# A selective-scan layer in front of an attention layer: softplus as ln(1 + exp), a new order of the steps' parts, and the second layer's weights loaded earlier

## The chip, the cores and the metric

The kernel runs on one core of a Trainium2 chip. The metric is the device time of one execution in microseconds; for the kernel before it is the median of three runs. A profile is one further execution, recorded instruction by instruction. Engines are named as in the profile: PE is the matrix engine, PEld its weight load, DVE the vector engine, ACT the scalar engine with its function tables, POOL the general engine, SP the engine that issues the DMAs. [...]

## The reference, cut to what matters

All arrays are float32. `x` has 4 images of 384 channels and 64 x 64 pixels.

```python
# layer 0: group norm, layer norm, a Mamba block, residual
xz = xn @ in_proj_w.T;  xb, z = split(xz)             # 384 -> 2 * 768
xc = silu(causal_conv4(xb) + conv_b)                  # per channel, 4 taps
x_dbl = xc @ x_proj_w.T                               # 24 (dt), 16 (B), 16 (C)
dt = softplus(x_dbl_dt @ dt_w.T + dt_b)
h = exp(dt * A) * h + (dt * xc) * B                   # 768 channels x 16 states, over 4096 pixels
y = (sum_n(h * C) + xc * D) * silu(z)
x = x + y @ out_proj_w.T
# layer 1: group norm, outlook attention, residual
a = softmax((avgpool2(xg) @ attn_w.T + attn_b) * scale)   # 12 heads, 9 x 9
v = conv_w[k] @ patches                                # 9 taps, stride 2
x = x + fold(a @ v) @ proj_w.T + proj_b
```

Since softplus(v) is ln(1 + e^v), the third line from `xc` can be had from either.

## The kernel before

The first layer cuts each image's 4096 pixels into 17 chunks of 241 (the last has 240), 68 chunks in all. A chunk has 12 units (`NU`), a unit being two groups of 32 channels with their 16 states each, laid out over 128 partitions. The main loop of `mamba_layer` goes over steps `s`; in step `s` unit `s` is scanned, and every unit's work is spread over the steps around it:

- `s_fetch(s + 4)`, in even steps: SP fetches dt and dt * xc, replicated over partitions, for two units, out of DRAM (`dtd`, `dxd`).
- `s_inputs2(s + 1)`: DVE multiplies half of the inputs by B (`bp`, in PSUM). `s_inputs(s + 2)`: POOL does the other half.
- `s_gate(s - 3)`, in even steps: DVE multiplies the finished output `y` into `zs`. `y` has one PSUM buffer, so the next pair of units may only write it after this.
- `s_scan(s, 0)` and `s_scan(s, 1)`: DVE's two scans. `s_decay(s + 1, 0)` and `(s + 1, 1)`: ACT's four exps each, into the PSUM tile that the scan of that number has just read. `s_carry(s + 1)`: ACT copies the carried state into `h`. `s_save(s)`: DVE saves the state.
- `s_outputs(s - 1)`: POOL multiplies `h` by C. `s_sum(s - 2)`: PE adds over the states, and in the first of two units also xc * D.

Around this the dense parts of other chunks are issued. Those ahead of the scan are named `f_...` (load, layer norm, projections `f_x` and `f_z`, `f_conv`, the silus in `f_gates`, `f_bc` and `f_xd` for x_dbl, `f_dt`, the softplus, `f_dtx`), those after it `e_...` (load of the residual, three output projections, store). Where each stands is written out by hand in two tables, `plan` (line 440) and `ends` (line 465): the key is a step relative to the chunk and one of six places in the step, EARLY, READY, SCAN, POOL, MID, LATE. A chunk's own units are scanned in relative steps 24 to 35, so relative step 13 falls into step 1 of the chunk before, -11 into step 1 as well, and so on; in what follows, steps are numbered 0 to 11 in this sense. A part's instructions go to the end of each engine's queue at its place. In `f_x`, `f_z`, `f_conv`, `f_dt` and `e_project` the matmuls and the ACT instruction that empties the PSUM tile are issued together, so ACT waits for PE if PE isn't done. All these matmuls share one PSUM tag of two buffers (`mm`).

ACT needs a table of functions for each of silu, softplus and exp; where the next function isn't in the loaded table, an ACT_TABLE_LOAD is put ahead of it.

The second layer, `outlook_layer`, runs when the first is done. It loads its own weights at its start (lines 726 to 731) into a pool that it opens there, then goes over 32 tiles of 8 rows.

Of the kernel before, what the change touches and what calls it, by code (L numbers as in the profile page):

```python
# [10 lines left out]
P = 128  # L11
C = 384
# [12 lines left out]
KK = 9  # L25
GW = 11


# [55 lines left out]
@with_exitstack  # L84
def mamba_layer(ctx, tc, x, w, x1, sc1, bi1, consts):

# [17 lines left out]
    small = ctx.enter_context(tc.tile_pool(name="small", bufs=2))  # L104
    io = ctx.enter_context(tc.tile_pool(name="io", bufs=3))
    front = ctx.enter_context(tc.tile_pool(name="front", bufs=1))
    cross = ctx.enter_context(tc.tile_pool(name="cross", bufs=2))
# [7 lines left out]

    def load(name, shape):
        t = wp.tile(shape, F32, tag=name, name=name)
        sp.dma_start(t, w[name])
        return t
# [10 lines left out]
    def x_load(b, i):  # L130
        if i == 0:
            xstats[b] = small.tile([P, NCB, NX, 6], F32, tag="xst", name="xst", bufs=1)
        xs = io.tile([P, NCB, XT], F32, tag="xt", name="xs")
        sp.dma_start(xs, x[b, :, i * XT : (i + 1) * XT].rearrange("(p cb) l -> p cb l", cb=NCB))
        return xs
# [35 lines left out]

    avg = load("avg", [P, P])
    for i in range(NX):
# [5 lines left out]

    onesc = load("onesc", [P, 1])  # L180
    lnw = load("lnw", [P, NCB])
    lnb = load("lnb", [P, NCB])
    win = load("win", [P, NCB, 2 * DI])
    cw = load("cw", [P, NJ, KC])
    cbias = load("cbias", [P, NJ])
    wx = load("wx", [P, NJ, 2 * NS + RK])

    KX = 2 * NS + RK + 1
    xd = wp.tile([2 * CG, TM], F32, tag="xd", name="xd")
    gp.memset(xd, 1.0)  # L190
    wdt = wp.tile([KX, DI], F32, tag="wdt", name="wdt")
    sp.dma_start(wdt[2 * NS :, :], w["wdt"])
# [4 lines left out]

    cdiag = wp.tile([P, NJ, KC, P], F32, tag="cdiag", name="cdiag")
    ddiag = wp.tile([P, NJ, P], F32, tag="ddiag", name="ddiag")
# [5 lines left out]

    sel = wp.tile([2 * NS, NG // 2, P], F32, tag="sel", name="sel")
    sp.dma_start(sel, w["sel"])
    pw = pmm.tile([P, 2, TM], F32, tag="mm", name="pw")
    for j in range(2 * NJ):
        for cb in range(NCB):  # L210
# [6 lines left out]
            )  # L217
    bxz = wp.tile([P, 2 * NJ], F32, tag="bxz", name="bxz")
# [3 lines left out]
    cws = wp.tile([P, NJ], F32, tag="cws", name="cws")  # L222
    ve.reduce_sum(cws, cw, AX.X)
    ve.tensor_mul(cws, cws, bxz[:, :NJ])
    ve.tensor_add(cbias, cbias, cws)
    pad = wp.tile([P, NJ], F32, tag="pad", name="pad")
# [17 lines left out]
    def f_load(c):  # L244
        c.xt = io.tile([P, NCB, XT], F32, tag="xt", name="xt")
# [125 lines left out]
    def f_gates(c):  # L371
        t = c.t
        ae.activation(c.xc[:, :, :t], c.xc[:, :, :t], AF.Silu)
        ae.activation(c.zs[:, :, :t], c.zs[:, :, :t], AF.Silu)

    def f_bc(c):
# [29 lines left out]
    def f_softplus(c):  # L406
        t = c.t
        ae.activation(c.dt[:, :, :t], c.dt[:, :, :t], AF.Softplus)
        c.bc = []
        for k in range(2):  # L410
            m = cross.tile([P, NG, TM], F32, tag=f"bc{k}", name=f"bc{k}")
            for r in range(4):
                sp.dma_start(
                    m[CG * r : CG * (r + 1), :, :t], c.bcd[k, :, r, :t].unsqueeze(0).to_broadcast([CG, NG, t])
                )
            c.bc.append(m)
        c.dtd = dram.tile([NJ, P, TM], F32, tag="dtd", name="dtd")
        sp.dma_start(c.dtd[:, :, :t].rearrange("j p t -> p j t"), c.dt[:, :, :t])

# [44 lines left out]

    ends = {
        (-3, MID): [lambda c: e_load(c)],
        (2, LATE): [lambda c: e_project(c, 0)],
        (4, LATE): [lambda c: e_project(c, 1)],
        (5, LATE): [lambda c: e_project(c, 2)],
        (8, READY): [lambda c: e_store(c)],  # L470
    }

    def parts(s, when):

        for k in range(s // NU + 3, s // NU - 2, -1):
# [133 lines left out]
    def e_load(c):  # L609
        c.xr = io.tile([P, NCB, XT], F32, tag="xr", name="xr", bufs=2)  # L610
        sp.dma_start(
            c.xr[:, :, : c.t], x[c.b, :, c.t0 : c.t0 + c.t].rearrange("(p cb) l -> p cb l", cb=NCB)
        )

    def e_project(c, cb):
# [5 lines left out]
        ae.copy(c.xr[:, cb, :t], po[:, 0, :t])  # L621

    def e_store(c):
# [5 lines left out]
        sp.dma_start(x1[c.b, :, c.t0 : c.t0 + t].rearrange("(p cb) l -> p cb l", cb=NCB), c.xr[:, :, :t])  # L629
        if c.t0 + t == L:  # L630
# [7 lines left out]

    pending = {}
    for s in range(-3 * NU, NU * (len(chunks) + 2)):  # L640
        k, m = divmod(s, NU)
# [20 lines left out]
        for i in range(2):  # L662
            if (u := unit(s)) is not None:
                s_scan(u, i)
            if i == 1:
                parts(s, SCAN)
                if u is not None:
                    s_save(u)
            if (u := unit(s + 1)) is not None:
                s_decay(u, i)  # L670
                if i == 0:
                    s_carry(u)
        if (u := unit(s - 1)) is not None:
            s_outputs(u)
# [8 lines left out]
        if u is not None and u.first:  # L683
            s_sum(u)
        parts(s, LATE)


@with_exitstack
def outlook_layer(ctx, tc, x1, w, out, sc1, bi1, consts):

# [21 lines left out]

    wp = ctx.enter_context(tc.tile_pool(name="wp1", bufs=1))
    io = ctx.enter_context(tc.tile_pool(name="io1", bufs=3))
# [4 lines left out]
    pt = ctx.enter_context(tc.tile_pool(name="pt", bufs=1, space=bass.MemoryType.PSUM))  # L719

    def load(name, shape):
        t = wp.tile(shape, F32, tag=name, name=name)
        sp.dma_start(t, w[name])
        return t
# [8 lines left out]
    ve.tensor_scalar_mul(wa, wa, 0.25)  # L733

# [239 lines left out]


@with_exitstack
def layers(ctx, tc, w, out):
# [16 lines left out]
    consts = (blk12, ident, eps, one)  # L994
    mamba_layer(tc, x.rearrange("b c h w -> b c (h w)"), w, x1, sc1, bi1, consts)
    outlook_layer(tc, x1, w, out, sc1, bi1, consts)

# [65 lines left out]
```

## Time and profile before

| | |
|---|---|
| time, median of 3 runs | 7237.03 us (7232.6 to 7237.15) |
| the profiled execution's own time | 7234.33 us |
| its span, from first to last instruction | 7232.5 us |
| busy: PE, DVE, ACT, POOL | 6332.4, 5651.4, 4972.4, 5426.5 us |
| mean granted PE clock | 0.912 |
| first scan, last scan pair | 139.1 us, 5925.9 us |
| table loads | 272, 1283 ns in the mean |

In the profile's lines of groups and waits, an output stands before `<-` and its inputs behind it, with buffer numbers left out; `h<-da,h` is the scan, `h<-st` the carry, `st` the saved state, `dt<-dt` the softplus. Lines of the program are of no use for telling instructions apart here, since all are recorded in one helper (L40). In a line of waits the numbers are the total in us, how often, and the longest. In a line of the timeline they are the start and the length in us, and a bracket at the end says how long the engine had been idle and what released it. A line of windows gives the stretch, its length, then busy us of PE, PEld, DVE, ACT and POOL with the number of instructions in parentheses, the granted PE clock, the DMA engines' busy share and GB/s.

### The profile page before, as it was taken

The numbers are of one execution on the slowest core, as the hardware profiler recorded it, in microseconds if no ns is written. First come the engines' busy times: TensorE is split into PE (matmuls) and PEld (weight loads), VectorE is DVE, ScalarE is ACT, GpSimd is POOL, SyncE is SP. The second block draws the span as 40 slices with busy tenths as digits, with TensorE's granted clock in tenths as the row PEclk, the third lists the DMA queues.
The fourth block names the chain that finished last, engine by engine and source line by source line (L and its number), as shares of the span: only waits on it lengthen the run. The fifth ranks groups of instructions, "written<-read, shape, count | busy, mean of one in ns | idle before, by whom it ended". The sixth has DMA issues, their size and how long they took to land.

```text
span 7232.5 us, 112296 instructions
## 1 busy us (share of the span) xinstructions
PE 6332.4 (88%) x40440; PEld 4261.8 (59%) x40440; DVE 5651.4 (78%) x5688; ACT 4972.4 (69%) x10729; POOL 5426.5 (75%) x2102
## 2 busy tenths in 40 slices
PE   6888888888888888888888888888888858999999
PEld 5566666566566666566566665566566634555555
DVE  4888888889888888888888888888888874444544
ACT  3777777777777777777777777777777754554454
POOL 3888888888888888888888888888888872433343
PEclk9889899898898999889889999889889979999999
DMA  4555444444554444444554444444554434445444
GB/s 115 127 125 125 114 113 106 116 110 121 126 128 112 117 109 106 117 117 120 126 123 112 114 109 106 111 113 110 117 119 111 110 104 150 164 167 173 163 162 151
DMA packets 899555, 893.17 MB, mean 123 GB/s; under 512 B 121706, under 2 KB 858780, under 8 KB 898485
## 3 DMA queue, kind: packets, MB, share of 16 engines
q1 hardware_dynamic: 898996, 886.00, 47.5%
q8 instruction: 318, 5.21, 0.3%
q14 instruction: 241, 1.97, 0.1%
HBM read 659.99 MB, written 225.68 MB: 122 GB/s over the span
## 4 chain that ended last, share of the span: by engine, by line
PE 54%; DVE 24%; ACT 13%; issue 4%; DMA 2%; POOL 2%; SPq 0%; DVEq 0%; ACTq 0%; POOLq 0%
DVE h L40 19%; PE y L40 14%; PE ps_in L40 11%; PE ps_cv L40 8%; ACT da L40 6%; PE psv L40 5%; PE ps_out L40 4%; PE pso L40 4%; PE ps L40 3%; PE psa L40 2%; POOL h L40 2%; ACT L40 2%; ACT xc L40 2%; ACT zs L40 1%; PE ps_dt L40 1%
## 5 line engine op out<-in xcount | busy, mean ns | idle before, releaser
L40 POOL TENSOR_TENSOR h<-h,bc 128x1928 f32<-128x1928 f32 (+1 forms) x816 | 3229.7, 3958 | 828.1 <-DVE st L40 661.0
L40 DVE TENSOR_TENSOR_SCAN h<-da,h 128x968 f32<-128x968 f32 (+1 forms) x1632 | 3451.8, 2156 | 505.4 <-ACT h L40 480.5
L40 ACT ACTIVATE da<-dtr,aneg 128x241 f32<-128x241 f32 (+1 forms) x6528 | 3038.2, 465 | 658.1 <-DVE h L40 362.1
L40 POOL TENSOR_TENSOR h<-dxr,bc 128x964 f32<-128x964 f32 (+1 forms) x816 | 1685.0, 2065 | 12.6 <-DMA dxr<-dxd 11.2
L40 PE MATMUL y<-h,ssum 128*32 128x241 f32 (+1 forms) x13056 | 1638.2, 410 | 0.6 <-POOL h L40 0.6
L40 PEld LDWEIGHTS y<-h,ssum 128*32 128x32 f32 x13056 | 736.5, 120 | 796.7 <-issue 438.4
L40 PE MATMUL ps_in<-u,win 128*128 128x241 f32 (+1 forms) x4896 | 1073.4, 373 | 5.5 <-DVE u L40 4.8
L40 POOL TENSOR_TENSOR bd<-ain,own 99x1188 f32<-99x1188 f32 x192 | 412.8, 2178 | 791.7 <-DMA ain<-ad 618.9
L40 PEld LDWEIGHTS ps_in<-u,win 128*128 128x128 f32 x4896 | 923.8, 192 | 140.1 <-issue 60.3
L40 DVE TENSOR_TENSOR h<-dxr,bp 128x964 f32<-128x964 f32 (+1 forms) x816 | 940.3, 1152 | 51.9 <-PE bp L40 31.8
L40 PE MATMUL y<-xc,ddiag 128*128 128x241 f32 (+1 forms) x816 | 327.8, 490 | 557.7 <-DVE zs L40 557.7
L40 PE MATMUL ps_cv<-xb,cdiag 128*128 128x241 f32 (+1 forms) x3264 | 718.1, 373 | 1.2 <-ACT xc L40 1.2
L40 PEld LDWEIGHTS ps_cv<-xb,cdiag 128*128 128x128 f32 x3264 | 601.7, 189 | 120.2 <-ACT da L40 51.4
L40 PE MATMUL psv<-wv,xp 128*128 128x384 f32 x1728 | 587.9, 492 | 0.9 <-ACT vst L40 0.8
L40 PE MATMUL ps_out<-zs,wout 128*128 128x241 f32 (+1 forms) x2448 | 585.7, 392 | 0.0
L40 PEld LDWEIGHTS y<-xc,ddiag 128*128 128x128 f32 x816 | 159.5, 229 | 665.2 <-issue 466.9
L40 PEld LDWEIGHTS ps_out<-zs,wout 128*128 128x128 f32 x2448 | 508.9, 208 | 51.7
L40 ACT ACTIVATE bd<-ain,own 99x324 f32<-99x324 f32 x704 | 334.6, 555 | 294.3 <-PE ps L40 282.6
L40 DVE TENSOR_TENSOR fold<-fold,ps 128x192 f32<-128x192 f32 (+1 forms) x768 | 211.2, 303 | 336.2 <-PE ps L40 323.0
L40 PEld LDWEIGHTS psv<-wv,xp 128*128 128x128 f32 x1728 | 320.5, 190 | 224.4 <-issue 7.8
L40 PE MATMUL ps_dt<-xd,wdt 25*128 25x241 f32 (+1 forms) x816 | 270.8, 478 | 166.8 <-ACT xd L40 166.8
L40 ACT ACTIVATE zs<-ps_in,bxz 128x241 f32<-128x241 f32 (+1 forms) x408 | 166.0, 459 | 329.5 <-PE ps_in L40 329.5
(98 smaller groups left out, 5385.3 us busy)
## 6 DMA issues: line engine op xcount, KB each, us to landing
dxr<-dxd SPq DMA_DIRECT2D x1536, 120.5 KB
dtr<-dtd SPq DMA_DIRECT2D x1536, 120.5 KB
bc<-bcd SPq DMA_DIRECT2D x512, 120.5 KB
vin<-vd SPq DMA_DIRECT2D x384, 148.5 KB
vd<-vst SPq DMA_DIRECT2D x96, 576.0 KB
dtd<-dt SPq DMA_DIRECT2D x64, 723.0 KB
dxd<-dtx SPq DMA_DIRECT2D x64, 723.0 KB
xs<-in_x SPq DMA_DIRECT2D x64, 384.0 KB
```

What stands on the lines that cost most here:

```text
L40: return self.tc.keep_in_program_order(issue(*args, **kwargs))
```

## The change

Four things change.

1. `f_dt` evacuates its PSUM tiles with Exp in place of a copy, and `f_log`, in place of the softplus, takes ln(dt + 1). A table set that has both exp and ln (`EXP_LN`) is loaded behind the silus and stays until the next ones.
2. `plan` and `ends` have other places. The loads of B and C for a chunk (`bc0`, `bc1`) stand in a part of their own, `f_spread`; the store of dt goes with the log. `e_load` comes 7 steps earlier.
3. In each step the carry is issued ahead of the first decay.
4. The pools that only the fronts use (`wf`, `iof`, `front`) stand on the right side of the memory and are closed in step `front_end`, the last before the last chunk's scan. From that step on each step issues one DMA of the second layer's weights, ten in all (`behind`), into the room that came free. `outlook_layer` gets them ready.

```diff
@@ f_gates
         ae.activation(c.xc[:, :, :t], c.xc[:, :, :t], AF.Silu)
         ae.activation(c.zs[:, :, :t], c.zs[:, :, :t], AF.Silu)
+        ae.preload_act_table_set(EXP_LN)
@@ f_dt
-        ae.copy(c.dt[:, 2 * jj : 2 * jj + 2, :t], pp[:, :, :t])
-
-    def f_softplus(c):
-        t = c.t
-        ae.activation(c.dt[:, :, :t], c.dt[:, :, :t], AF.Softplus)
+        ae.activation(c.dt[:, 2 * jj : 2 * jj + 2, :t], pp[:, :, :t], AF.Exp)
+
+    def f_log(c):
+
+        t = c.t
+        ae.activation(c.dt[:, :, :t], c.dt[:, :, :t], AF.Ln, bias=one)
+        c.dtd = dram.tile([NJ, P, TM], F32, tag="dtd", name="dtd")
+        sp.dma_start(c.dtd[:, :, :t].rearrange("j p t -> p j t"), c.dt[:, :, :t])
+
+    def f_spread(c):
+
+        t = c.t
         c.bc = []
...
-        c.dtd = dram.tile([NJ, P, TM], F32, tag="dtd", name="dtd")
-        sp.dma_start(c.dtd[:, :, :t].rearrange("j p t -> p j t"), c.dt[:, :, :t])
@@ plan
-        (-12, MID): [f_load],
-        (-11, MID): [f_mean],
-        (-10, READY): [f_center],
-        (-10, LATE): [f_square],
-        (-7, LATE): [f_var],
-        (-6, EARLY): [f_root],
-        (-6, POOL): [f_pow],
-        (-5, MID): [f_rs],
-        (-5, LATE): [f_scale],
-        (7, MID): [at(f_x, 0)],
-        (8, LATE): [at(f_x, 1), at(f_z, 0)],
-        (9, LATE): [at(f_x, 2), at(f_z, 1)],
-        (10, LATE): [at(f_conv, 0)],
-        (11, LATE): [at(f_conv, 1), at(f_z, 2)],
-        (12, LATE): [at(f_conv, 2), f_gates],
-        (14, MID): [f_bc],
-        (14, LATE): [f_xd],
-        (15, LATE): [at(f_dt, 0), at(f_dt, 1)],
+        (-12, READY): [f_load],
+        (-11, SCAN): [f_mean],
+        (-11, POOL): [f_center],
+        (-8, EARLY): [f_square],
+        (-8, LATE): [f_var],
+        (-7, MID): [f_root],
+        (-5, EARLY): [f_pow],
+        (-5, READY): [f_rs],
+        (-5, POOL): [f_scale],
+        (6, POOL): [at(f_x, 0)],
+        (7, POOL): [at(f_conv, 0)],
+        (7, MID): [at(f_z, 0)],
+        (8, SCAN): [at(f_x, 1)],
+        (9, LATE): [at(f_z, 1)],
+        (10, SCAN): [at(f_x, 2)],
+        (10, LATE): [at(f_z, 2)],
+        (12, READY): [at(f_conv, 1)],
+        (12, MID): [at(f_conv, 2)],
+        (13, POOL): [f_gates],
+        (14, LATE): [f_bc],
+        (15, EARLY): [f_xd],
+        (16, EARLY): [at(f_dt, 0)],
+        (16, READY): [at(f_dt, 1)],
         (16, LATE): [at(f_dt, 2)],
-        (17, LATE): [f_softplus],
-        (18, SCAN): [f_dtx],
-        (22, MID): [f_b],
+        (17, EARLY): [f_log],
+        (18, MID): [f_spread],
+        (19, READY): [f_dtx],
+        (22, SCAN): [f_b],
@@ ends
-        (-3, MID): [lambda c: e_load(c)],
-        (2, LATE): [lambda c: e_project(c, 0)],
-        (4, LATE): [lambda c: e_project(c, 1)],
-        (5, LATE): [lambda c: e_project(c, 2)],
-        (8, READY): [lambda c: e_store(c)],
+        (-10, MID): [lambda c: e_load(c)],
+        (2, MID): [lambda c: e_project(c, 0)],
+        (6, EARLY): [lambda c: e_project(c, 1)],
+        (6, MID): [lambda c: e_project(c, 2)],
+        (13, MID): [lambda c: e_store(c)],
@@ the main loop
             if (u := unit(s + 1)) is not None:
-                s_decay(u, i)
                 if i == 0:
                     s_carry(u)
+                s_decay(u, i)
...
+        if s == front_end:
+            fronts.close()
+        if s >= front_end:
+            behind()
@@ outlook_layer
-    wa = load("wa", [P, NCB, NA])
-    ab = load("ab", [P, NA])
-    wv = load("wv", [P, NCB, KK, C])
-    wpr = load("wpr", [P, NCB, NCB, P])
-    pb = load("pb", [P, NCB])
-    own = load("own", [GW * KK, GW])
...
+def outlook_weights(ctx, tc, w, weights):
...
+    for name in ("wa", "wv"):
+        for cb in range(NCB):
+            sp.dma_start(weights[name][:, cb], w[name][:, cb])
+            yield
+    for name in ("ab", "wpr", "pb", "own"):
+        sp.dma_start(weights[name], w[name])
+        yield
```

The places of `ends` are relative to the step after the chunk's own last unit, 36, so (6, EARLY) is step 6.

More of the change, by code (lines that the diff above doesn't have):

```diff
@@ L1 @@
+from contextlib import ExitStack
 import concourse.bass as bass
@@ L26 @@
 GW = 11
+EXP_LN = "natural_log_exp_and_others"
 class InOrder:
@@ L84, in mamba_layer @@
 @with_exitstack
-def mamba_layer(ctx, tc, x, w, x1, sc1, bi1, consts):
+def mamba_layer(ctx, tc, x, w, x1, sc1, bi1, consts, behind):
     nc = tc.nc
@@ L104, in mamba_layer @@
     small = ctx.enter_context(tc.tile_pool(name="small", bufs=2))
-    io = ctx.enter_context(tc.tile_pool(name="io", bufs=3))
-    front = ctx.enter_context(tc.tile_pool(name="front", bufs=1))
+    io = ctx.enter_context(tc.tile_pool(name="io", bufs=2))
+    fronts = ExitStack()
+    wf = fronts.enter_context(tc.tile_pool(name="wf", bufs=1, side="right"))
+    iof = fronts.enter_context(tc.tile_pool(name="iof", bufs=3, side="right"))
+    front = fronts.enter_context(tc.tile_pool(name="front", bufs=1, side="right"))
     cross = ctx.enter_context(tc.tile_pool(name="cross", bufs=2))
@@ L114, in mamba_layer, with load @@
     py = ctx.enter_context(tc.tile_pool(name="py", bufs=1, space=bass.MemoryType.PSUM))
-    def load(name, shape):
-        t = wp.tile(shape, F32, tag=name, name=name)
+    def load(name, shape, pool=wp):
+        t = pool.tile(shape, F32, tag=name, name=name)
         sp.dma_start(t, w[name])
@@ L132, in x_load @@
             xstats[b] = small.tile([P, NCB, NX, 6], F32, tag="xst", name="xst", bufs=1)
-        xs = io.tile([P, NCB, XT], F32, tag="xt", name="xs")
+        xs = iof.tile([P, NCB, XT], F32, tag="xt", name="xs")
         sp.dma_start(xs, x[b, :, i * XT : (i + 1) * XT].rearrange("(p cb) l -> p cb l", cb=NCB))
@@ L170, in norm_part @@
                 norms.pop(0)
-    avg = load("avg", [P, P])
+    avg = load("avg", [P, P], wf)
     for i in range(NX):
@@ L177, in mamba_layer @@
         norm_part()
[L180 to L186, printed above, removed]
+    onesc = load("onesc", [P, 1], wf)
+    lnw = load("lnw", [P, NCB], wf)
+    lnb = load("lnb", [P, NCB], wf)
+    win = load("win", [P, NCB, 2 * DI], wf)
+    cw = load("cw", [P, NJ, KC], wf)
+    cbias = load("cbias", [P, NJ], wf)
+    wx = load("wx", [P, NJ, 2 * NS + RK], wf)
     KX = 2 * NS + RK + 1
-    xd = wp.tile([2 * CG, TM], F32, tag="xd", name="xd")
+    xd = wf.tile([2 * CG, TM], F32, tag="xd", name="xd")
     gp.memset(xd, 1.0)
-    wdt = wp.tile([KX, DI], F32, tag="wdt", name="wdt")
+    wdt = wf.tile([KX, DI], F32, tag="wdt", name="wdt")
     sp.dma_start(wdt[2 * NS :, :], w["wdt"])
@@ L196, in mamba_layer @@
     wout = load("wout", [P, NJ, NCB, P])
-    cdiag = wp.tile([P, NJ, KC, P], F32, tag="cdiag", name="cdiag")
+    cdiag = wf.tile([P, NJ, KC, P], F32, tag="cdiag", name="cdiag")
     ddiag = wp.tile([P, NJ, P], F32, tag="ddiag", name="ddiag")
@@ L203, in mamba_layer @@
         gp.tensor_scalar(ddiag[:, j, :], ident, dvec[:, j : j + 1], None, ALU.mult)
-    sel = wp.tile([2 * NS, NG // 2, P], F32, tag="sel", name="sel")
+    sel = wf.tile([2 * NS, NG // 2, P], F32, tag="sel", name="sel")
     sp.dma_start(sel, w["sel"])
@@ L217, in mamba_layer @@
             )
-    bxz = wp.tile([P, 2 * NJ], F32, tag="bxz", name="bxz")
+    bxz = wf.tile([P, 2 * NJ], F32, tag="bxz", name="bxz")
     ve.tensor_copy(bxz, pw[:, 0, : 2 * NJ])
@@ L221, in mamba_layer @@
         ve.tensor_scalar(win[:, cb, :], win[:, cb, :], lnw[:, cb : cb + 1], None, ALU.mult)
-    cws = wp.tile([P, NJ], F32, tag="cws", name="cws")
+    cws = wf.tile([P, NJ], F32, tag="cws", name="cws")
     ve.reduce_sum(cws, cw, AX.X)
@@ L225, in mamba_layer @@
     ve.tensor_add(cbias, cbias, cws)
-    pad = wp.tile([P, NJ], F32, tag="pad", name="pad")
+    pad = wf.tile([P, NJ], F32, tag="pad", name="pad")
     ve.tensor_scalar_mul(pad, bxz[:, :NJ], -1.0)
+    ae.preload_act_table_set(EXP_LN)
     aneg = wp.tile([P, NQ, NG], F32, tag="aneg", name="aneg")
@@ L244, in f_load @@
     def f_load(c):
-        c.xt = io.tile([P, NCB, XT], F32, tag="xt", name="xt")
+        c.xt = iof.tile([P, NCB, XT], F32, tag="xt", name="xt")
         sp.dma_start(
@@ L374, in f_gates @@
         ae.activation(c.zs[:, :, :t], c.zs[:, :, :t], AF.Silu)
+        ae.preload_act_table_set(EXP_LN)
     def f_bc(c):
@@ L440, in mamba_layer @@
     plan = {
[L441 to L458 removed]
+        (-12, READY): [f_load],
[21 more added lines that the diff above has]
+        (16, READY): [at(f_dt, 1)],
         (16, LATE): [at(f_dt, 2)],
[L460 to L462 removed]
+        (17, EARLY): [f_log],
+        (18, MID): [f_spread],
+        (19, READY): [f_dtx],
+        (22, SCAN): [f_b],
     }
     ends = {
[L466 to L470 removed]
+        (-10, MID): [lambda c: e_load(c)],
[3 more added lines that the diff above has]
+        (13, MID): [lambda c: e_store(c)],
     }
     def parts(s, when):
[L475 removed]
+        for k in range(s // NU + 3, s // NU - 4, -1):
             if 0 <= k < len(chunks):
@@ L609, in e_load @@
     def e_load(c):
-        c.xr = io.tile([P, NCB, XT], F32, tag="xr", name="xr", bufs=2)
+        c.xr = io.tile([P, NCB, XT], F32, tag="xr", name="xr")
         sp.dma_start(
@@ L621, in e_project, with e_write @@
         ae.copy(c.xr[:, cb, :t], po[:, 0, :t])
+    def e_write(c):
+        t = c.t
+        sp.dma_start(x1[c.b, :, c.t0 : c.t0 + t].rearrange("(p cb) l -> p cb l", cb=NCB), c.xr[:, :, :t])
     def e_store(c):
@@ L628, in e_store @@
             ve.bn_stats(st1[c.b][:, cb, c.ci, :], c.xr[:, cb, :t])
-        sp.dma_start(x1[c.b, :, c.t0 : c.t0 + t].rearrange("(p cb) l -> p cb l", cb=NCB), c.xr[:, :, :t])
+        e_write(c)
         if c.t0 + t == L:
@@ L639, in mamba_layer @@
     pending = {}
+    front_end = NU * (len(chunks) - 1) - 1
     for s in range(-3 * NU, NU * (len(chunks) + 2)):
@@ L685, in mamba_layer, with outlook_layer @@
         parts(s, LATE)
+        if s == front_end:
+            fronts.close()
+        if s >= front_end:
+            behind()
 @with_exitstack
-def outlook_layer(ctx, tc, x1, w, out, sc1, bi1, consts):
+def outlook_layer(ctx, tc, x1, w, out, sc1, bi1, consts, weights):
     nc = tc.nc
@@ L711, in outlook_layer @@
     )
-    wp = ctx.enter_context(tc.tile_pool(name="wp1", bufs=1))
+    wp = ctx.enter_context(tc.tile_pool(name="zero1", bufs=1))
+    wa, ab, wv, wpr, pb, own = (weights[name] for name in ("wa", "ab", "wv", "wpr", "pb", "own"))
+    ve.tensor_scalar_mul(wa, wa, 0.25)
     io = ctx.enter_context(tc.tile_pool(name="io1", bufs=3))
@@ L719, in outlook_layer @@
     pt = ctx.enter_context(tc.tile_pool(name="pt", bufs=1, space=bass.MemoryType.PSUM))
[L721 to L724, printed above, removed]
-    wa = load("wa", [P, NCB, NA])
-    ab = load("ab", [P, NA])
-    wv = load("wv", [P, NCB, KK, C])
-    wpr = load("wpr", [P, NCB, NCB, P])
-    pb = load("pb", [P, NCB])
-    own = load("own", [GW * KK, GW])
-    ve.tensor_scalar_mul(wa, wa, 0.25)
     zero = wp.tile([KK, C], F32, tag="zero", name="zero")
@@ L973, in outlook_layer @@
                 p_pixels(new)
+def outlook_weights(ctx, tc, w, weights):
+    wp = ctx.enter_context(tc.tile_pool(name="wp1", bufs=1, side="right"))
+    sp = InOrder(tc, tc.nc.sync)
+    na = HEADS * KK * KK
+    shapes = {
+        "wa": [P, NCB, na],
+        "ab": [P, na],
+        "wv": [P, NCB, KK, C],
+        "wpr": [P, NCB, NCB, P],
+        "pb": [P, NCB],
+        "own": [GW * KK, GW],
+    }
+    for name, shape in shapes.items():
+        weights[name] = wp.tile(shape, F32, tag=name, name=name)
+    for name in ("wa", "wv"):
[5 more added lines that the diff above has]
+        yield
 @with_exitstack
@@ L994, in layers @@
     consts = (blk12, ident, eps, one)
-    mamba_layer(tc, x.rearrange("b c h w -> b c (h w)"), w, x1, sc1, bi1, consts)
-    outlook_layer(tc, x1, w, out, sc1, bi1, consts)
+    weights = {}
+    later = outlook_weights(ctx, tc, w, weights)
+    mamba_layer(
+        tc, x.rearrange("b c h w -> b c (h w)"), w, x1, sc1, bi1, consts, lambda: next(later, None)
+    )
+    for _ in later:
+        pass
+    outlook_layer(tc, x1, w, out, sc1, bi1, consts, weights)
 def layouts(inputs):
```

## The prediction

> **What bounds the kernel now.** I read the page's totals first, then busy times and waits of the steady part of the first layer (300 to 5800 us), then the timeline of one chunk.
>
> ```profile
> PE 6332.4 (88%) x40440; PEld 4261.8 (59%) x40440; DVE 5651.4 (78%) x5688; ACT 4972.4 (69%) x10729; POOL 5426.5 (75%) x2102
> PEclk9889899898898999889889999889889979999999
> ```
>
> ```profile
> 300.00:5800.00 5500.00, 4789.09 (x26806) 3328.29 (x26803) 4733.91 (x4187) 4129.92 (x8989) 4658.19 (x1674) 0.90 0.48 115
> ```
>
> No engine is full. The 816 scan pairs start between 139.1 and 5925.9 us; over 65 steady chunks the mean period is 85.5 us for 12 steps, so 5500 us hold 64.4 chunks. Per chunk (columns PE, weight load, DVE, ACT, POOL): PE 74.4, DVE 73.5, ACT 64.1, POOL 72.3 us. What else goes into 85.5 us are waits:
>
> ```profile
> DVE h L40 <- ACT h L40: 463.8, 259, 5.2
> DVE vs L40 <- PE ps_var L40: 201.6, 63, 5.7
> ACT zs L40 <- PE ps_in L40: 312.9, 193, 1.9
> ACT xc L40 <- PE ps_cv L40: 229.6, 191, 2.2
> PE y L40 <- DVE zs L40: 496.2, 128, 7.4
> ```
>
> DVE waits 7.2 us a chunk for ACT (decays and carry late) and 3.1 us for the variance matmuls; smaller waits bring it to 11.4. ACT in turn stands behind matmuls whose evacuation was queued just behind them. The median distances between the scan starts of steps 0, 1, ... 11 and the next, read off DVE's timeline, are 7.65, 11.06, 5.46, 5.73, 5.51, 9.35, 6.85, 7.55, 5.51, 6.72, 6.72, 6.82 us. About 5.5 us is DVE's minimum, so time is lost at 0, 1 and 5. The gates are the loss at step 1:
>
> ```profile
> 3046.36 4.24 DVE L40 TENSOR_TENSOR_SCAN h<-da,h 128x968 f32<-128x968 f32 x2 [2.04 <-ACT h L40]
> ...
> 3049.07 0.81 ACT L40 ACTIVATE xc<-ps_cv,cbias 128x241 f32<-128x241 f32 x2 [0.96 <-PE ps_cv L40]
> 3049.90 1.28 ACT L40 ACT_TABLE_LOAD   x1
> ...
> 3053.92 1.28 ACT L40 ACT_TABLE_LOAD   x1
> ...
> 3057.40 4.24 DVE L40 TENSOR_TENSOR_SCAN h<-da,h 128x968 f32<-128x968 f32 x2 [4.19 <-ACT h L40]
> ```
>
> The softplus is different: its two loads cost ACT the same, but the next scan pair (3091.19) has no idle time, since DVE was busy with dtx.
>
> ```profile
> 3083.93 1.28 ACT L40 ACT_TABLE_LOAD   x1
> ...
> 3085.23 1.41 ACT L40 ACTIVATE dt<-dt 128x1446 f32<-128x1446 f32 x1
> ...
> 3086.90 1.28 ACT L40 ACT_TABLE_LOAD   x1
> ...
> 3088.50 1.64 DVE L40 TENSOR_TENSOR dtx<-dt,xc 128x1446 f32<-128x1446 f32 x1
> ...
> 3091.19 4.23 DVE L40 TENSOR_TENSOR_SCAN h<-da,h 128x968 f32<-128x968 f32 x2
> ```
>
> PE idles in the same chunk, then runs slowly (the fifth and later columns are DVE, ACT, POOL; the clock is the third from the end):
>
> ```profile
> 3065.00:3079.00 14.00, 13.79 (x42) 8.79 (x43) 13.93 (x14) 9.20 (x22) 13.70 (x6) 0.53 0.71 143
> ...
> 3092.00:3098.00 6.00, 0.00 (x0) 0.00 (x0) 5.97 (x7) 4.44 (x12) 6.00 (x3) 0.77 0.88 216
> 3098.00:3105.00 7.00, 6.97 (x31) 4.33 (x32) 6.97 (x10) 3.90 (x10) 5.90 (x3) 0.71 0.83 210
> ```
>
> A mean clock of 0.90 is half speed for 20% of the time, 17 us a chunk. PE was busy nearly throughout those stretches, so some 7 of its 74.4 us are lost there: 67 us at full clock.
>
> [...] The trace has 272 loads (4 a chunk) of 1283 ns mean; [...] softplus and silu both took 1411 ns for 1446 elements. [...] Here the idle 6 us were followed by such a stretch, but so were 2.5 us (3062.5 to 3065)[...].
>
> **The change, part by part.**
>
> Tables. Exp replaces the copy out of PSUM at the same width: 0 (555 ns[...]). Ln replaces softplus: 1411 ns[...]. Two of four loads go: 2 x 1.283 = 2.57 us of ACT a chunk, 175 us in all. But softplus's loads lay beside dtx, so by themselves they are worth between 0 and 175 us, nearer to 0; what they give is room for ACT's other waits. If dtx's cover were gone they would be worth the whole 2.57.
>
> Places. I walk one chunk with t = first scan of a step. DVE: two scans 4.24, save 0.17, the B product 1.15 = 5.46 seen at free steps; gate 0.40 at even steps. POOL: 3.94 + 2.07 = 6.01 a step, its C product starting after the save at t + 4.4, and the B product of a unit on DVE waits for POOL's for that unit. ACT: decays of 1.96 behind each scan, done at t + 6.4; the next are due at the next t + 2.1. The carry goes ahead of the decays into ACT's wait: 0.19 off the late path, nothing elsewhere.
> - 0 to 1: both convolutions were multiplied while step 11, which has no front work, ran; ACT finds them ready: POOL sets 5.75 (now 7.65).
> - 1 to 2: DVE does center 0.97 and the statistics of the store 1.02 here: 5.45 + 0.97 + 1.02 + 0.40 = 7.84. The gates (1.28 + 1.41 + 1.39 + 1.28 = 5.36) now come behind both decays: t1 + 6.4 to t1 + 11.8, that is t2 + 3.9. The next decays end at t2 + 5.9: 2 to 3 is 6.0. Together 13.8, now 16.5.
> - 3 to 4: x_dbl's matmuls stand behind the output projection 0, which waits for the gate at t2. 3.2 + 2.4 + 2.6 us later ACT, queued at the copy to xd ahead of the decays, goes on: t3 + 2.3 at full clock, t3 + 5 at half. I take 7.0 (bounds 5.85 and 7.8).
> - 4 to 5, 5 to 6: the square and two exps fill ACT up to t4 + 3.9: 5.9. Then the log is 1.41: 6.1. The variance is done long before its root asks (now 3.1 us of wait).
> - 6 to 7: dtx 1.65 ahead of the scan: 7.3. 7 to 8: scale and gate 6.8.
> - 8 to 9: projection 1 can take its PSUM buffer only when the root has read it (t5 + 4.5), after 4.9 us of PE idleness. From there PE has projections 1 and 2, two front projections, a convolution, two sums and the rs: 20 us, so the first z is ready at t8 + 4.5, ACT is held, and the step is 5.45 + 1.9 = 7.35.
> - 9, 10, 11: 6.3, 5.6, 6.4 (x statistics, gates, POOL; the last z is just hidden).
> Sum: 5.75 + 7.84 + 6.0 + 7.0 + 5.9 + 6.1 + 7.3 + 6.8 + 7.35 + 6.3 + 5.6 + 6.4 = 78.3 us. If the 4.9 us idle halve the clock for 7 us, that adds 3.2 to the z's delay; my rows for PE add up to 71.5 against 67, so 1.3 of it isn't there. I add 1.7: **80 us a chunk** against 85.5.
>
> SP. The eight bc loads move to step 18, dtd's store is ahead of them, dxd's store moves to step 19. Fetch 20 waits for dxd (6 us at most now), lands by about t7 + 13, and POOL wants it at t7 + 20: hidden, with 7 us to spare. The store of x1 and its load wait on work long done.
>
> Second layer. Now its weights are issued at 5951.72, the zero stores queue behind 5.2 MB of wv, and the first load of x1 waits for those:
>
> ```profile
> 5971.36 2.25 SPq L40 DMA_DIRECT2D xr<-x  x3
> 5976.54 3.81 ACT L40 ACTIVATE xp<-xr,bi,sc 128x372 f32<-128x372 f32 x6 [30.68 <-DMA xr<-x]
> ```
>
> With the weights there, the zeros follow the scaling of wa (1.68) at about 5954, x1's load about 3 us later, the pixels about 5962: 15 us less. The 7.7 MB take some 30 us of DMA time (estimate: 216 GB/s at a share of 0.88) within ten steps that have no front traffic; delaying a fetch there can cost up to 10 us, or nothing.
>
> Sum: 66 intervals x 5.5 = 363, plus 15, is 378. The profiled execution took 7234.3 us (span 7232.5, 1.8 around it), 2.7 under the median of three: 7237 - 378 = 6859. Prologue and second layer's loop are unchanged.
>
> **Rivals.**
> - Floor: PE keeps its clock, no z is late; POOL and DVE in lockstep give 77: 8.5 x 66 + 15 = 576, 6660 us. For it: DVE's content is 73.5. Against: the 4.9 us hole. 0.18.
> - PE late: half clock at both holes, ACT held at xd and z: 83 us, 2.5 x 66 + 15 = 180, 7057 us. That is also what the two loads alone would give (175). 0.20.
> - Slower: PE becomes the bound. 67 us at full clock plus 6 idle leaves 12.5 us before 85.5: from 25 us of half clock a chunk (now 17) the chunk is longer than now. At 32 us it is 89: 3.5 x 66 - 15 = 216 more, 7450 us. For it: heavy steps 0, 6, 7 follow empty ones. Against: PE has more work per time. 0.06.
> - No difference, since the waits only move: 0.02.
> My forecast, 78 to 82 us a chunk, has 0.54. Without the slower case, the "same" and some of the outer halves of the two neighbours, 8 in 10 lie between 6670 and 7090. A measurement of this kernel tells 0.2% (14 us) from no change. Faster 0.92, same 0.02, slower 0.06.
>
> **What would show it.** 136 table loads; DVE's wait for ACT's carry down from 463.8 to under 200 us and for ps_var near 0; steps 1 and 5 at 8 and 6 us; step 8 above 7 with ACT waiting for ps_in; a new PE wait ahead of ps_out for the root; pixels of the second layer about 12 us after the first layer's last statistics. It is wrong if steps 3 or 8 exceed 9 us, if the clock falls under 0.88, or if POOL waits for dxr.

## The result, and the profile after

The changed kernel takes **6619.5 us** (median of 4 runs, 6618.7 to 6624.5) against 7236.8 us before: a ratio of 0.915, 95% interval 0.9134 to 0.9166, that is 617 us less. The prediction had 6859 us and a range down to 6670. The direction, and most of what moves, were right; the gain is 1.6 times the predicted one, and the time lies below the case called "floor" (6660).

The page's busy times and granted clock, and below them the first layer's steady part in the line of windows (300 to 5300 us):

```profile
PE 6139.8 (93%) x40440; PEld 4209.5 (64%) x40440; DVE 5656.6 (85%) x5688; ACT 4789.1 (72%) x10594; POOL 5505.0 (83%) x2102
...
PEclk9999999999999999999999999999999889999999
```

```profile
300.00:5300.00 5000.00, 4651.28 (x27130) 3301.03 (x27126) 4828.48 (x4265) 4015.90 (x9003) 4825.17 (x1705) 0.94 0.53 130
```

Over the same 65 chunks the mean period is 76.35 us (before 85.49), so these 5000 us hold 65.5 chunks. DVE and POOL are busy for 96.6% and 96.5% of the stretch; before it was 86% and 85%. DVE is busy for about as long a chunk as before (73.7 us, before 73.5): the waits went. DVE's and ACT's waits in that stretch:

```profile
ACT zs L45 <- PE ps_in L45: 203.9, 102, 3.6
...
DVE h L45 <- ACT da L45: 66.6, 79, 2.1
...
DVE zs L45 <- PE y L45: 56.1, 58, 3.6
```

The wait for ACT's carry (463.8 us) is now one of 66.6 us for its decays, the one for the variance (201.6 us) isn't in the list any more. DVE's wait for the sum that its gate reads (`zs <- y`) has grown, from 14.2 us to 56.1. The silus, on the timeline of one chunk:

```profile
3067.13 1.28 ACT L45 ACT_TABLE_LOAD   x1
3067.92 0.40 DVE L45 TENSOR_TENSOR zs<-y,zs 128x241 f32<-128x241 f32 x1
3068.24 4.22 DVE L45 TENSOR_TENSOR_SCAN h<-da,h 128x968 f32<-128x968 f32 x2
...
3071.15 1.28 ACT L45 ACT_TABLE_LOAD   x1
...
3074.96 4.24 DVE L45 TENSOR_TENSOR_SCAN h<-da,h 128x968 f32<-128x968 f32 x2 [1.20 <-ACT da L45]
```

The same two loads and two silus that left DVE idle for 4.19 us now leave 1.20, since DVE has a scan pair to do meanwhile. At the change of layers, from the last statistics of the first layer to the first pixels of the second, in the kernel before (whose line of the first pixels, at 5976.54, the prediction shows) and in the changed one:

```profile
5945.90 0.41 DVE L40 BATCH_NORM_STATS2 st<-xr 128x6 f32<-128x240 f32 x1 [2.43 <-ACT xr L40]
```

```profile
5345.51 0.41 DVE L45 BATCH_NORM_STATS2 st<-xr 128x6 f32<-128x240 f32 x1 [2.43 <-ACT xr L45]
...
5359.32 3.82 ACT L45 ACTIVATE xp<-xr,bi,sc 128x372 f32<-128x372 f32 x6 [13.85 <-DMA xr<-x]
```

It is 13.8 us, before it was 30.6. The distances of scan starts, step by step, read off DVE's timeline (means over 65 chunks), beside what the prediction's walk through one chunk had:

| step to the next | 0 | 1 | 2 | 3 | 4 | 5 | 6 | 7 | 8 | 9 | 10 | 11 | sum |
|---|---|---|---|---|---|---|---|---|---|---|---|---|---|
| before | 7.50 | 11.05 | 5.46 | 6.12 | 5.50 | 9.08 | 7.23 | 7.82 | 5.57 | 6.92 | 6.47 | 6.77 | 85.49 |
| walk | 5.75 | 7.84 | 6.0 | 7.0 | 5.9 | 6.1 | 7.3 | 6.8 | 7.35 | 6.3 | 5.6 | 6.4 | 78.3 + 1.7 |
| after | 5.52 | 7.59 | 6.65 | 6.09 | 5.52 | 5.97 | 8.16 | 7.63 | 5.55 | 6.26 | 5.58 | 5.83 | 76.35 |

(80.0 - 76.35) x 66 intervals is 241 us, the whole miss of 240. Its largest parts are three: step 8 (1.80 us a chunk), the 1.7 added for the clock, and step 3 (0.91). Steps 6 and 7 went the other way (0.86 and 0.83), and so did step 2 (0.65); the rest is in small differences.

### The profile page after: what moved, and what is told of

The parts are those of the page before. It is cut to its first block, busy times and chain, and to the rows that moved or that the text cites. A ratio compares the mean times of both kernels' runs of the same rounds, so it can differ in the third digit from the quotient of the medians.

```text
span 6616.9 us, 112259 instructions
## 1 busy us (share of the span) xinstructions
PE 6139.8 (93%) x40440; PEld 4209.5 (64%) x40440; DVE 5656.6 (85%) x5688; ACT 4789.1 (72%) x10594; POOL 5505.0 (83%) x2102
## 4 chain that ended last, share of the span: by engine, by line
PE 39%; DVE 38%; ACT 10%; issue 5%; DMA 4%; POOL 3%; SPq 1%; DVEq 0%; POOLq 0%; ACTq 0%
DVE h L45 31%; PE y L45 9%; PE psv L45 5%; PE ps_out L45 5%; PE ps_in L45 4%; PE pso L45 4%; ACT da L45 4%; PE ps_cv L45 3%; PE ps L45 3%; PE psa L45 3%; POOL h L45 2%; ACT L45 2%; DVE dtx L45 1%; ACT xc L45 1%; PE ps_var L45 1%
## 5 line engine op out<-in xcount | busy, mean ns | idle before, releaser
L45 POOL TENSOR_TENSOR h<-dxr,bc 128x964 f32<-128x964 f32 (+1 forms) x816 | 1702.1, 2086 | 40.8 <-DMA dxr<-dxd 24.1
L45 PE MATMUL y<-h,ssum 128*32 128x241 f32 (+1 forms) x13056 | 1580.8, 401 | 1.3 <-POOL h L45 1.3
L45 PEld LDWEIGHTS y<-h,ssum 128*32 128x32 f32 x13056 | 716.9, 117 | 744.2 <-issue 376.4
L45 PE MATMUL ps_cv<-xb,cdiag 128*128 128x241 f32 (+1 forms) x3264 | 701.5, 371 | 21.6 <-DVE u L45 19.6
L45 PE MATMUL ps_out<-zs,wout 128*128 128x241 f32 (+1 forms) x2448 | 565.9, 377 | 63.2 <-DVE zs L45 63.2
L45 PEld LDWEIGHTS ps_out<-zs,wout 128*128 128x128 f32 x2448 | 478.9, 198 | 127.7 <-DVE zs L45 86.2
L45 PE MATMUL y<-xc,ddiag 128*128 128x241 f32 (+1 forms) x816 | 279.6, 428 | 136.4 <-DVE zs L45 136.4
L45 PE MATMUL ps_dt<-xd,wdt 25*128 25x241 f32 (+1 forms) x816 | 224.0, 410 | 93.8 <-ACT xd L45 89.1
```

The source lines that it names most:

```text
L45: return self.tc.keep_in_program_order(issue(*args, **kwargs))
```

## Two things that the trace of after shows

**Projection 1 doesn't wait for the root.** PE's and DVE's instructions around it in the changed kernel:

```profile
3013.67 1.10 PE L45 MATMUL ps_out<-xr,ident 128*128 128x241 f32 x2 [0.19 <-ACT dt L45]
...
3016.49 0.21 DVE L45 TENSOR_SCALAR vs<-ps_var 121x1 f32<-121x1 f32 x2
```

The projection begins 2.8 us before the root reads the variance, right behind the exp that empties dt's tile. So it didn't take the variance's buffer, the one two allocations back, but the other one, dt's, which is released earlier in the program's order.

**dtx is either 1.66 us or far longer.** dtx is dt * xc. A usual chunk, and one in which it comes up 0.38 us behind the start of POOL's C product:

```profile
3023.11 2.47 POOL L45 TENSOR_TENSOR vs<-vs,mhalf 121x1 f32<-121x1 f32 x2
...
3023.52 1.66 DVE L45 TENSOR_TENSOR dtx<-dt,xc 128x1446 f32<-128x1446 f32 x1
```

```profile
2945.07 3.97 POOL L45 TENSOR_TENSOR h<-h,bc 128x1928 f32<-128x1928 f32 x1
2945.45 5.11 DVE L45 TENSOR_TENSOR dtx<-dt,xc 128x1446 f32<-128x1446 f32 x1
```

In the first, POOL's two pows take 2.47 us in place of 1.1 (the median of one was 0.55 before) and the second ends 0.4 us after dtx, which takes its usual time; in the second the C product takes its usual time (3.97 us, the median is 3.94) and dtx ends 1.5 us after it. It is so throughout the trace: 52 of 68 dtx take 1.66 to 1.70 us, 16 take 4.5 to 7.8, and each of these 16 ends 1.5 us behind POOL's work, 12 behind a C product and 4 behind the B product that followed it. By these times dtx and POOL's product run one after the other. DVE's own B product, which reads one input out of PSUM, isn't held so: in the changed kernel it took 1.10 to 1.19 us all 816 times, 810 of them beside an instruction of POOL. What makes the difference isn't shown. The prediction had dtx at a fixed 1.65, though the trace of before had longer ones, 20 of 68 over 2.2 us:

```profile
L40 DVE TENSOR_TENSOR dtx<-dt,xc x68: 1632/1641/3176, 114.7 to 5824.0; 128x1446 f32<-128x1446 f32 x64, 128x1440 f32<-128x1440 f32 x4
```

(The three numbers are the shortest, median and longest in ns.)

The theory for the experiments: the places carry the gain by taking DVE's waits away; the tables by themselves give nothing, since the freed loads lie beside dtx; and how late DVE comes to step 7 decides whether dtx meets a C product. The rivals: tables and places add up, each by its own us; or the long dtx are a symptom and cost nothing of their own.

## The experiments

Each was timed beside the kernel before (medians of 7235.5 to 7238.4 us in three sets); ratios are to it, differences are between medians.

### The tables alone, the places alone, and all but the tables

On the kernel before, `e1_tables`:

```diff
+        ae.preload_act_table_set(EXP_LN)          # behind the silus
...
-        ae.copy(c.dt[:, 2 * jj : 2 * jj + 2, :t], pp[:, :, :t])
+        ae.activation(c.dt[:, 2 * jj : 2 * jj + 2, :t], pp[:, :, :t], AF.Exp)
...
-        ae.activation(c.dt[:, :, :t], c.dt[:, :, :t], AF.Softplus)
+        ae.activation(c.dt[:, :, :t], c.dt[:, :, :t], AF.Ln, bias=one)
```

> Of the change only the tables: Exp out of PSUM, ln(1 + exp), two loads a chunk in place of four; all places as before. Theory (the softplus's loads lie beside dtx on DVE, so the freed 2.57 us of ACT a chunk are mostly not on the path): 7150 to 7230 us, likeliest 7190, with 136 or 137 loads. Rival (every load is on the path): 7236 - 68 x 2.57 = 7062 us.

Measured 7238.7 us, ratio 1.000 (0.9991 to 1.0009): nothing, where the theory had a small gain (7150 to 7230). The timeline at the log, in the place where the softplus had stood:

```profile
3090.05 1.97 ACT L43 ACTIVATE da<-dtr,aneg 128x241 f32<-128x241 f32 x4 [0.42 <-DVE h L43]
3091.95 0.19 ACT L43 COPY h<-st 128x8 f32<-128x8 f32 x1
3091.99 1.64 DVE L43 TENSOR_TENSOR dtx<-dt,xc 128x1446 f32<-128x1446 f32 x1
...
3094.69 4.23 DVE L43 TENSOR_TENSOR_SCAN h<-da,h 128x968 f32<-128x968 f32 x2
```

ACT now waits for the scan (0.42 us) where it had loaded a table, and the next pair comes at DVE's pace as before. The loads at the silus, which do stand on the path, stay.

`e11_places` is the changed kernel without the rest (softplus, late carry; the second layer's weights come behind the first layer's last step, but SP issues most of them before it ends, as in `e3_weights_late` below). `e2_softplus` is the changed kernel with only the tables taken back:

```diff
-        ae.preload_act_table_set(EXP_LN)
...
-        ae.activation(c.dt[:, 2 * jj : 2 * jj + 2, :t], pp[:, :, :t], AF.Exp)
+        ae.copy(c.dt[:, 2 * jj : 2 * jj + 2, :t], pp[:, :, :t])
...
-        ae.activation(c.dt[:, :, :t], c.dt[:, :, :t], AF.Ln, bias=one)
+        ae.activation(c.dt[:, :, :t], c.dt[:, :, :t], AF.Softplus)
```

> Of the change only the new places of the parts; softplus, the order of decay and carry, and the second layer's loads as before. Theory (the places carry most of the gain, and step 5, where the softplus now stands alone with its two loads, has about 1 us of ACT slack, so the loads cost 1.6 us a chunk): 6620 + 66 x 1.6 + 17 = 6743, with the carry up to 6770 us. Rival (tables and places are worth half each): 6930 us.

> The changed kernel with the softplus back (copy out of PSUM, softplus at the log's place, four loads a chunk). Theory (1.6 us a chunk of the 2.57 come onto the path at step 5): 6725 us. Rivals: all of it is on the path, 6620 + 175 = 6795 us; none is, 6620 us.

Measured 6859.6 us (0.9478, 0.9464 to 0.9492) and 6856.2 us (0.9473, 0.9457 to 0.9489). The places alone give 378 us; the tables, worth nothing alone, give 237 on top of them. Both expectations were 90 to 130 us too low, and 237 is more than the 175 us that the two loads a chunk last: something besides ACT's time was paid. In `e2_softplus` steps 5 and 6 take 8.33 and 10.07 us, against 5.97 and 8.16.

### Keeping the C product behind dtx

`e6_dtx_guard` on the changed kernel; `e14_softplus_guard` is the same on `e2_softplus`:

```diff
         ve.tensor_mul(dtx[:, :, :t], c.dt[:, :, :t], c.xc[:, :, :t])
+        seen = front.tile([1, 1], F32, tag="seen", name="seen")
+        gp.tensor_copy(seen, dtx[:1, NJ - 1, t - 1 : t])
```

> The changed kernel with a POOL copy of one element of dtx issued right behind dtx, so that POOL's next C product can't start ahead of dtx. Theory (16 dtx are held 3 to 6 us behind a C product): these go, the copy and POOL's wait cost some 0.3 us a chunk: 6570 to 6600 us, no dtx above 3.5 us. Rival (POOL is as full as DVE, and its waits cost what DVE's cost): 6620 to 6660 us.

> The run with the softplus in the new places (6856 us, four loads a chunk), with the POOL copy behind dtx added, so that no C product of POOL can start ahead of dtx. Theory (of the 237 us that the two loads cost there, more than the 175 us that they last, the larger part is that ACT's delay lets dtx come up behind the C product, 64 of 68 times): the long dtx go and the time falls by 130 to 190 us, to 6665 to 6725 us. Rival (the delay itself is the cost, and dtx would have waited for ACT's decays anyway): 6820 us or more.

Measured 6564.5 us (0.9072, 0.9057 to 0.9087), 5.5 below the theory's range, and 6665.6 us (0.9211, 0.9196 to 0.9227), at the lower end of it. The dtx of the four kernels, from the view of that tile: `e2_softplus`, then `e14_softplus_guard`, then the changed kernel, then `e6_dtx_guard`:

```profile
L45 DVE TENSOR_TENSOR dtx<-dt,xc x68: 1665/4526/7331, 117.6 to 5462.9; 128x1446 f32<-128x1446 f32 x64, 128x1440 f32<-128x1440 f32 x4
```

```profile
L45 DVE TENSOR_TENSOR dtx<-dt,xc x68: 1651/1659/1666, 117.7 to 5273.1; 128x1446 f32<-128x1446 f32 x64, 128x1440 f32<-128x1440 f32 x4
```

```profile
L45 DVE TENSOR_TENSOR dtx<-dt,xc x68: 1656/1658/7756, 116.7 to 5223.5; 128x1446 f32<-128x1446 f32 x64, 128x1440 f32<-128x1440 f32 x4
```

```profile
L45 DVE TENSOR_TENSOR dtx<-dt,xc x68: 1646/1658/2660, 115.6 to 5167.5; 128x1446 f32<-128x1446 f32 x64, 128x1440 f32<-128x1440 f32 x4
```

With the softplus 64 of 68 are long; all durations add up to 307.4 us, with the copy behind dtx to 112.8: 195 us less, and the kernel is 191 us faster. In the changed kernel it is 178.2 and 113.9: 64 us less, and 55 us faster. So the long dtx are paid nearly in full, which rules out the rival that they cost nothing. Without them the tables are worth 6665.6 - 6564.5 = 101 us, 1.5 us a chunk of the 2.57. Step 5 is then 8.32 us with the softplus, 5.93 without, while step 7 is 0.8 us shorter. `e6_dtx_guard` is faster than the kernel before and than the changed one.

`e9_pow_early` goes the other way and takes the short pow out of the moment when dtx comes up:

```diff
-        (-5, EARLY): [f_pow],
+        (-6, POOL): [f_pow],
```

> The changed kernel with POOL's pow one step earlier (step 6, behind the C product), so that POOL goes from its B product straight to the C product when dtx comes up on DVE. Theory (dtx, [...] in most chunks gets in only because the short pow is running then): dtx takes 4.5 us or more in most of the 68 chunks in place of 16, about 52 x 3.4 = 177 us more, 6790 us. Rival (the long dtx have another cause, the pow is just moved): 6610 to 6630 us.

Measured 6673.5 us (0.9221, 0.9208 to 0.9235), 54 us slower than the changed kernel, a third of what the theory expected. Long dtx rose only from 16 to 25:

```profile
L45 DVE TENSOR_TENSOR dtx<-dt,xc x68: 1645/2204/8446, 116.3 to 5278.7; 128x1446 f32<-128x1446 f32 x64, 128x1440 f32<-128x1440 f32 x4
```

But nearly all are held a little, and half of the 68 take 2.2 us or more. The sum of all dtx, 249.7 us, is 71 more than in the changed kernel. So POOL's products do hold dtx, but the theory took the pow to be needed. Counted in the timelines: in the changed kernel 48 of the 52 short dtx begin while POOL runs a pow alone; here 50 of 68 come up while a B product runs, and 41 of these wait for its remainder (2.23 us at most with their own time) and get in ahead of the C product. The other 9, and 16 that come up beside a C product, are the long ones.

### The wait that the prediction had assumed

`e5_root_gate` puts it in:

```diff
     def e_project(c, cb):
...
+        if cb == 1 and rooted:
+            vs, n = rooted.pop()
+            pe.matmul(po[:1, 1, 0:1], vs[:n, 1:2], ident[:n, 0:1], start=True, stop=True)
```

where `f_root` leaves its output in `rooted`.

> The changed kernel with one matmul of one column ahead of output projection 1 that reads the root's output, so that PE waits there for DVE's root, which is the wait that the prediction had assumed for the PSUM buffer. Its product goes to a part of the bank that nobody reads. Theory of the prediction (z late, ACT held in step 8): step 8 from 5.5 to 7.3 or more, 1.9 to 3.7 us a chunk, 6745 to 6865 us. Rival (PE's rows add up to more than its real work, and the backlog is gone by step 7): under 6645 us.

Measured 6740.0 us (0.9312, 0.9298 to 0.9326): 120 us slower, 1.9 us a chunk, just below the theory's range. PE's wait in one chunk, and the wait of DVE in the steady part that grew (56.1 us in the changed kernel):

```profile
3009.49 0.21 DVE L45 TENSOR_SCALAR vs<-ps_var 121x1 f32<-121x1 f32 x2
3009.85 0.19 PE L45 MATMUL ps_out<-ident,vs 120*1 120x1 f32 x2 [2.17 <-DVE vs L45]
```

```profile
DVE zs L45 <- PE y L45: 131.7, 64, 3.0
```

So such a wait does cost time, but neither where the walk put it nor all that it put: step 8 stays at 5.54 us. Step 7 grows from 7.63 to 8.65, where DVE's gate waits for the sum that PE does behind the convolution, and steps 5 and 6 by 0.49 and 0.43. PE is held for the root in 27 chunks, by 45.5 us in all and 3.1 at most, where the walk had 4.9 us of idleness in each. The time at half clock rises from 12.6% of the steady stretch to 15.9%. There are also 26 long dtx in place of 16, worth 25 of the 120 us.

### The cover of the silus

`e10_store_step8` takes 1.02 us of DVE's work out of step 1:

```diff
-        (13, MID): [lambda c: e_store(c)],
+        (8, READY): [lambda c: e_store(c)],
```

> The changed kernel with the store of x1 and its statistics (1.02 us of DVE) back in step 8, where they stood before, so that only the center and a gate cover the silus in step 1. Theory (DVE's sum stays, step 1 loses cover that the silus need): step 1 shorter by 1.0, the step after it longer by about as much, step 7 longer by 1.0, in all 0.5 to 1.0 us a chunk: 6650 to 6690 us. Rival (POOL sets those steps in any case): 6610 to 6630 us.

Measured 6696.9 us (0.9254, 0.924 to 0.9268), 77 us slower, a little more than expected. Step 1 falls from 7.59 to 6.60, step 2 rises from 6.65 to 7.32, step 7 from 7.63 to 8.66, step 9 from 6.26 to 6.64. Two thirds of what step 1 gives up come back in the next step, where DVE waits for the decays behind the silus (66.6 us in the changed kernel):

```profile
DVE h L45 <- ACT da L45: 120.2, 78, 2.6
```

The store is paid in full in its other place. So in step 1 two thirds of it run in time that ACT needs anyway.

### The second layer's weights and the carry

`e3_weights_late` was to undo the early loads, by issuing the ten loads behind the last step:

```diff
-        if s == front_end:
-            fronts.close()
-        if s >= front_end:
-            behind()
...
-    for _ in later:
+    for _ in outlook_weights(ctx, tc, w, weights):
         pass
```

> The changed kernel with the second layer's weights issued at its start, as before. Theory: the distance from the last statistics to the first pixels goes from 13.8 back to 30 us: 6636 us. Rival (the early loads also slow the last chunks of the first layer): between 6620 and 6632 us.

Measured 6627.2 us (6617.7 to 6632.1). It doesn't undo them: SP reaches the large ones long before the first layer ends, and the pixels come as early as in the changed kernel (13.7 us behind the last statistics).

```profile
5310.56 1.35 SPq L45 DMA_DIRECT2D wa<-in_wa  x3
```

`e12_weights_own` loads them in `outlook_layer`, into its own pool, as before the change:

```diff
-    wa, ab, wv, wpr, pb, own = (weights[name] for name in (...))
...
+    wa = load("wa", [P, NCB, NA])
...
+    own = load("own", [GW * KK, GW])
```

> The changed kernel with the second layer's weights loaded by that layer itself, in its own pool, as before the change, and the fronts' pools kept to the end of the first layer. Theory: from the last statistics to the first pixels 30 us in place of 13.8: 6636 us. Rival (the early loads slow the last two chunks by as much as they save): 6615 to 6625 us.

Measured 6645.5 us (6627.7 to 6651.2), 26 us slower. The zeros again stand behind the weights, and x1 behind the zeros:

```profile
5355.92 0.37 SPq L45 DMA_DIRECT2D wa<-in_wa  x1
...
5375.98 2.28 SPq L45 DMA_DIRECT2D xr<-x  x3
5381.20 3.81 ACT L45 ACTIVATE xp<-xr,bi,sc 128x372 f32<-128x372 f32 x6 [30.68 <-DMA xr<-x]
```

From the last statistics (5350.55) it is 30.7 us, 16.8 more than in the changed kernel. In the profiled execution another 5 us come from the first layer, whose last scan pair starts at 5329.7 in place of 5324.6; the scatter of this kernel's runs is too wide to say more.

`e4_carry_late` puts the carry back behind the first decays:

```diff
+                s_decay(u, i)
                 if i == 0:
                     s_carry(u)
-                s_decay(u, i)
```

> The changed kernel with the carry behind the first decays again. Theory (the carry lies in ACT's wait for the scan; behind the decays it is on the path only in the step after the gates, and where the z comes late): 0.2 to 0.4 us a chunk, 6630 to 6650 us. Rival: it is hidden either way, 6615 to 6625 us; a small shift can also move dtx against the C product, by 3 us in each chunk where it does.

Measured 6625.7 us (6620.8 to 6634.5): 6 us above the changed kernel, whose runs reach to 6624.5. That isn't told apart; what there is goes with 21 long dtx in place of 16.

### The coefficients of the group norms

Three chunks of the changed kernel take 87 to 88.5 us, those in whose steps 7 to 11 the next image's coefficients are computed. `e8_guard_norms` starts these, and those of the second layer's finished images but the last, at step 3, on top of `e6_dtx_guard`:

```diff
-            if ci == NX // 2 and m == 6:
+            if ci == NX // 2 and m == 2:
...
+        if m == 2 and due_norms:
+            norms.append(due_norms.pop())
```

> As the run with the copy behind dtx, and the group norm coefficients of the next image (5 parts, now from step 7 on) and of the second layer's image (now from step 2 on) both start at step 3, where no part holds a PSUM buffer. Theory (three chunks with 87 to 88.5 us and three with 82 to 83 lose 8 to 13 us because a coefficient's tile holds one of the two buffers over a step): 40 to 50 us less than without it, 6520 to 6555 us. Rival (the loss is the coefficients' own DVE work): within 10 us of the run without it.

Measured 6581.5 us (0.9096, 0.9082 to 0.9109), 17 us slower than `e6_dtx_guard`. The theory fell: the three chunks take 88.1 us, against 85.2 in `e6_dtx_guard`. Steps 3 and 5 aren't free places, and ACT's wait for dt's matmuls rises from 19.5 to 79.2 us. What a good place is, and whether the held buffer is the cause at all, stays open.

## Why the prediction was wrong

What failed is the step "8 to 9: projection 1 can take its PSUM buffer only when the root has read it (t5 + 4.5), after 4.9 us of PE idleness". The buffer was assumed to be the one two allocations back. The trace shows the projection ahead of the root, and step 8 is 5.55 us where the walk had 7.35. The 1.7 us a chunk for a halved clock hung on the same idle time. Together the two terms are 3.5 us a chunk, 231 us. With that wait put in, the kernel is 120 us slower, half of the miss of 240, and step 8 still 5.54: so the walk also had the wrong size and place for what such a wait costs. Half clock fell from 20% of the steady stretch to 12.6% by the trace's record of the granted clock, and rose to 15.9% with the wait put in; that fewer gaps of PE are the whole reason isn't shown. The term of 1.7 also has a slip: 3.2 less 1.3 is 1.9, which would have put the forecast 13 us higher.

**Step 3** was put at 7.0 and is 6.09 us. The walk let the whole output projection wait for the last gate. The changed kernel's PE timeline:

```profile
3064.58 2.20 PE L45 MATMUL ps_out<-zs,wout 128*128 128x241 f32 x10
3068.37 0.68 PE L45 MATMUL ps_out<-zs,wout 128*128 128x241 f32 x2 [1.58 <-DVE zs L45]
...
3071.14 2.65 PE L45 MATMUL ps_xd<-xc,wx 128*56 128x241 f32 x12
```

Only the last of six channel groups waits, so by the walk's own terms (0.68 us behind the gate in place of 3.2) x_dbl is done some 2.5 us earlier, and ACT is hardly held at xd: 7.3 us in all over the steady stretch. Step 3's share is 0.91 x 66 = 60 us; no run tests this cause alone.

**Steps 6 and 7** were 0.86 and 0.83 us longer than the walk in the mean, 112 us in all, which hid part of the other errors. Step 6 is dtx with its long cases (65 us over 1.66 each in all): with the copy behind dtx it is 7.22, and its median is 7.09 anyway. Step 7 isn't dtx, for it stays at 7.79 with the copy. The walk had no wait there, but DVE's gate waits for PE's sum: nearly all of the 56.1 us shown above falls into this step, and with the copy it is 55.2.

**The tables.** "By themselves they are worth between 0 and 175 us, nearer to 0": 0, as `e1_tables` shows. "What they give is room for ACT's other waits" was right in kind, but in the new places it is 237 us, 136 more than the 101 that ACT's time accounts for, through dtx. Exp was 560 ns in place of 555. Ln was 1502, where the prediction had taken the softplus's 1411 for it: 91 ns more, in a call with a bias, which the softplus's call doesn't have; what the bias alone takes isn't shown. There were 137 loads; 136 were forecast. The steady part has 130, two a chunk, one ahead of the first silu and one behind the second; exp and ln both run between them without a load of their own.

**Silus, variance, store.** 1 to 3 was put at 13.8 us and is 14.2; step 5 at 6.1 and is 5.97; `e10_store_step8` shows the cover in step 1, for two thirds of the store.

**SP and the second layer.** Little was late behind SP in the steady part: POOL has three waits, 13.8 us in all, that the profile puts down to dxd or dxr. The prediction had named a wait for dxr as a sign of being wrong; there was one, of 5.3 us. The change of layers gained 16.8 us, against 15.

**Rivals.** "Floor" came nearest: DVE and POOL do run in lockstep, at 96.6 and 96.5% busy. It had taken 77 us, and 76.35 were measured with long dtx and coefficients in them; an undisturbed chunk takes 73.1 to 75.1. Its "no z is late" didn't hold in full, for ACT still waits 203.9 us for them, but step 8 isn't longer for it. "PE late" and "slower" were wrong: PE was 93% busy and held DVE for little more than the 56.1 us of the gate.

## What to carry to other kernels

A saving in one engine can be worth nothing alone and more than its own length beside another change: look for what a shift of the schedule sets off, such as an operation that then takes longer beside another engine's (here dtx, 4.5 to 7.8 us in place of 1.66). Where operations of two engines hold each other up, a tiny instruction that makes one of them wait for the other (here 191 and 55 us) can be cheaper than leaving it to chance who comes first. In a walk over a pool of two buffers, read off the trace which release a tile waits for, and in a group of matmuls let only those wait whose own input is late.

## What the runs showed of the hardware that I had not expected

- dtx took 1.66 us on DVE, or 4.5 to 7.8 us where it met a C product of POOL. It can be held twice in a row: the one that began at 2622.85 us ended at 2630.38, 3.61 us behind a C product of 3.95 us and 1.52 behind the B product of 2.15 that followed it.
- In the steady part of the kernel before, PE's clock was halved 136 times, for 3.4 to 13.7 us each by the trace's record. The stretch from 3064.49 to 3078.14 us began while PE stood idle for 2.48 us (from 3062.47). A gap isn't always there: in the changed kernel 46 of 129 such stretches begin after 5 us in which the profile has PE busy throughout (such as the one at 3011.16 us). What starts these stays open.
- A table load cost 1.28 us and nothing around it: in the chunk of the kernel before that the prediction shows, the loads begin 0.02 us behind the instruction of ACT ahead of them, and between their end and the next instruction there is no more than that.
